# A hybrid scan and attention kernel: other order in the head, a shifted pipeline in the scan loop, a fourth lane and fewer background steps at the end

## Chip, core and metric

The kernel runs on one core of one Trainium2 chip. Times are device microseconds (us) of one execution. A few executions of each kernel are taken, and the median is quoted with its range.

## The reference, cut to what matters

The input is four images of 64 x 64 positions with 96 channels. One layer takes signs of the inputs, projects, convolves 3 x 3, and runs a selective scan over the 4096 positions of an image in four directions, for 192 channels with 16 states each. A small attention and a quantised feed-forward part follow. The scan, simplified:

```python
delta = softplus(delta + delta_bias)
def step(h, inp):
    ut, dt, Bt, Ct = inp
    dA = exp(dt[..., None] * A)                       # decay
    h = dA * h + (dt * ut)[..., None] * Bt[:, :, None, :]   # injection
    y = einsum('bkdn,bkn->bkd', h, Ct)                # product, sum over the states
    return h, y
```

## The kernel before

The scan is cut into 1536 pieces of 128 rows (32 channels x 4 states) by 1024 positions: 4 images, 4 directions, 4 stretches of positions, 24 pieces for each. For a piece ScalarE (ACT) computes the decay, GpSimd (POOL) the injection, VectorE (DVE) the scan, DVE or POOL the product with C, and TensorE (PE) sums over the states. A tally of the microseconds given to DVE and POOL, kept when the program is built, decides which of them takes a product. SyncE (SP) issues nearly all loads and stores. This is the loop:

```python
AHEAD = 4
...
self.decay(0)
for i in range(AHEAD):
    self.inject(i)
for i in range(n):
    ...
    if i + 1 < n:
        self.decay(i + 1)                       # ACT
    if i % 8 == 3 and i > 8:
        self.evacuate(i - 4)                    # ACT: ys <- yp, then stores
    if i >= 3:
        self.reduce(i - 3)                      # PE: sums of y, three steps behind
    if i + AHEAD < n:
        self.inject(i + AHEAD)                  # POOL, four steps ahead; 9 buffers
    self.late_product()                         # POOL: product of piece i - 1
    self.scan(i)                                # DVE (and its product)
    ...
    if i % 8 == 3 and self.todo:
        ...
        lanes.append(self.prepare())            # delta of later pieces: PE, ACT, DVE, store
    interleave(lanes)
    next(back, None)                            # one step of background work
    if i > n - 64:
        next(back, None)                        # a second one near the end
```

`back` is background work in small steps: the next image's head (projections, convolution, rows), a transposition, and the epilogue of an image whose scans are done.

Three stretches run without a loop to fill them. The **head** is the first image's column sums, projections, convolution (16 parts), the rows that hold B, C and the signs, and the first deltas. The **tail** is the last image's epilogue: eight chunks of sums, of which some were done in the background, a small middle, and eight closing chunks in three lanes. A lane is a set of buffers in which one chunk is worked on beside those of the other lanes.

```python
more = [e.spare_lane(x) for x in range(2)]
drain([behind] + [e.sums(ln) for ln in more])
drain([e.middle()])
drain([e.last(ln) for ln in [e.lane] + more])
```

The signs (gT) that a preparation multiplies are loaded ahead, except for the first direction of the next image:

```python
if (b, k) not in self.gs:
    self.load_signs(b, k)                       # loaded where it is used
if (ci, part) == (NCH - 1, 0) and k != KORD[-1]:
    self.load_signs(b, KORD[KORD.index(k) + 1]) # loaded 24 pieces ahead
```

## Time and profile before

5511.64 us, median of three runs (5508.68 to 5516.53). The page of the profiled run begins with the busy time of each engine and its share of the span:

```profile
PE 3466.0 (63%) x20089; PEld 1360.3 (25%) x20089; DVE 4996.1 (91%) x3142; ACT 3631.0 (66%) x5673; POOL 4947.3 (90%) x2247
```

The groups of instructions between 280 and 5140 us show the work of one piece (line, engine, operation, tiles, count; busy us in all, mean ns of one; idle time before them by releaser):

```profile
L421 POOL TENSOR_TENSOR w<-dl,bc 128x1024 f32<-128x1024 f32 x1471 | 3429.1, 2358 | 72.3 <-PE yp L1409 51.0 <-issue 8.6 <-DMA bc<-bcd 8.4
L421 DVE TENSOR_TENSOR_SCAN dA<-dA,cy,w 128x1024 f32<-128x1024 f32 x691 | 1618.9, 2343 | 86.7 <-ACT dA L1336 71.5 <-ACT cy L1378 9.8 <-POOL w L421 5.2
L421 DVE TENSOR_TENSOR w<-dA,bc 128x1024 f32<-128x1024 f32 x928 | 1136.7, 1225 | 53.0 <-DVE dA L421 0.5 <-DMA bc<-bcd 0.3
```

Both engines are busy nine tenths of the span. The prediction works from these durations.

| stretch of the profiled run | us |
|---|---|
| head, to the first injection | 260.9 |
| to piece 96 | 582.0 |
| pieces 96 to 1440 | 4450.1 |
| pieces 1440 to 1535 | 349.8 |
| piece 1535 to the end | 122.3 |

A piece's time is read off as follows, here and below: the busy time of ACT's decays is summed in windows of 4 us, and piece N is where N/1536 of it is reached. This is good to some 2 us.

### The profile page before, as it was taken

To read this page: it belongs to the slowest core of one execution; us is meant where nothing else is said; L and a number is where in the kernel's file an instruction comes from. 1 tells how busy PE (TensorE), PEld (TensorE's weight loads), DVE (VectorE), ACT (ScalarE), POOL (GpSimd) and SP (SyncE) were. 2 spreads that over 40 slices of the span, in tenths; PEclk is the share of its full clock that TensorE was granted. 3 is DMA by queue.
4 is the path that set the end of the run, shared out by engine and by line. 5 is a ranking of instruction groups with operands and counts; after the bars stand their busy time and mean duration, and the time that the engine had idled before them with its cause. 6 is when DMAs were issued, how large, how long until landed. Compare 5 with 4: busy or idle time off the path is not lost. (4 is left out here: it accounts for less than half of the span.)

```text
span 5504.2 us, 62064 instructions
## 1 busy us (share of the span) xinstructions
PE 3466.0 (63%) x20089; PEld 1360.3 (25%) x20089; DVE 4996.1 (91%) x3142; ACT 3631.0 (66%) x5673; POOL 4947.3 (90%) x2247
## 2 busy tenths in 40 slices
PE   5456765467655776656665677664777664444677
PEld 2221222122222232222222222221232221111223
DVE  3299999999999999999999999999999999999884
ACT  4468776677766667777767666775656775655544
POOL 2199999899999999999999999999999999999981
PEclk7666876578867777768876787766787665556777
DMA  4455665766666666676765666666666565765642
GB/s 78 122 184 195 206 203 188 245 214 208 209 200 202 195 205 211 201 235 212 219 192 185 207 211 195 205 217 225 198 209 203 178 198 196 219 204 185 203 152 60
DMA packets 613659, 1069.84 MB, mean 194 GB/s; under 512 B 225147, under 2 KB 344468, under 8 KB 611540
## 3 DMA queue, kind: packets, MB, share of 16 engines
q1 hardware_dynamic: 612244, 1065.86, 61.3%
q8 instruction: 157, 2.57, 0.2%
q14 instruction: 170, 1.39, 0.1%
q10 hardware_dynamic: 1088, 0.02, 0.0%
HBM read 833.16 MB, written 229.35 MB: 193 GB/s over the span
## 5 line engine op out<-in xcount | busy, mean ns | idle before, releaser
L421 POOL TENSOR_TENSOR w<-dl,bc 128x1024 f32<-128x1024 f32 x1536 | 3580.9, 2358 | 155.5 <-PE yp L1409 72.6
L1336 ACT ACTIVATE dA<-dl,anm 128x1024 f32<-128x1024 f32 x1536 | 1714.5, 1116 | 474.4 <-DVE w L421 285.8
L421 DVE TENSOR_TENSOR_SCAN dA<-dA,cy,w 128x1024 f32<-128x1024 f32 x726 | 1700.9, 2343 | 90.7 <-ACT dA L1336 75.5
L1409 PE MATMUL yp<-w,sum 128*32 128x256 f32 x12288 | 1286.6, 514 | 384.8 <-POOL w L421 230.7
L421 POOL TENSOR_TENSOR w<-h,bc 128x1024 f32<-128x1024 f32 x573 | 1349.1, 2355 | 124.1 <-DVE h L421 110.0
L421 DVE TENSOR_TENSOR w<-dA,bc 128x1024 f32<-128x1024 f32 x963 | 1179.5, 1225 | 54.7 <-DVE dA L421 0.5
L421 DVE TENSOR_TENSOR_SCAN h<-dA,cy,w 128x1024 f32<-128x1024 f32 x426 | 996.7, 2340 | 16.0 <-ACT dA L1336 15.8
L1409 PEld LDWEIGHTS yp<-w,sum 128*32 128x32 f32 x12288 | 315.6, 128 | 1467.9 <-issue 690.1
L1378 ACT COPY cy<-dA 128x1 f32<-128x1 f32 x721 | 113.5, 157 | 772.5 <-DVE w L421 770.6
L421 DVE TENSOR_TENSOR_SCAN dA<-dA,w 128x1024 f32<-128x1024 f32 x237 | 540.9, 2282 | 36.7 <-ACT dA L1336 28.4
L1271 PE MATMUL dps<-gT,wdz 128*128 128x64 fp8e5 x1000 | 113.9, 313 | 358.8 <-ACT ys L1423 329.8
L421 DVE TENSOR_TENSOR_SCAN h<-dA,w 128x1024 f32<-128x1024 f32 x147 | 334.8, 2278 | 4.9 <-ACT dA L1336 3.4
L1284 PE MATMUL dps<-sp,ident 128*128 128x512 f32 x376 | 273.0, 815 | 46.0 <-ACT dps L1280 45.8
L1414 PE MATMUL yp<-ya,back 128*128 128x256 f32 x576 | 235.1, 528 | 4.5 <-DMA ya<-yd 2.5
L659 PE MATMUL cv<-tp,cwA 128*96 128x512 fp8e5 x576 | 198.4, 470 | 60.3 <-ACT r L706 55.1
L1271 PEld LDWEIGHTS <-wdz 128*128 128x128 fp8e5 x1024 | 95.4, 152 | 440.1 <-issue 409.7
L1271 PE MATMUL dps<-gT,wdy 128*128 128x64 fp8e5 x504 | 58.5, 317 | 205.2 <-ACT ys L1423 203.2
L1276 ACT ACTIVATE pd<-dps,dbias,pvd 128x512 f32<-128x512 f32 x188 | 143.3, 762 | 20.2 <-PE dps L1271 20.2
L1414 PEld LDWEIGHTS yp<-ya,back 128*128 128x128 f32 x576 | 122.6, 246 | 133.4 <-issue 93.5
L1378 ACT COPY cy<-h 128x1 f32<-128x1 f32 x431 | 79.9, 185 | 113.7 <-DVE h L421 112.8
L941 PE MATMUL yc<-eys,mean 96*96 96x512 f32 x240 | 132.1, 702 | 24.2 <-DVE vks L421 8.9
L1277 ACT ACTIVATE sp<-dps,dbias,pvd 128x512 f32<-128x512 f32 x188 | 144.2, 767 | 0.0
(312 smaller groups left out, 4433.1 us busy)
## 6 DMA issues: line engine op xcount, KB each, us to landing
dl<-dld SPq DMA_DIRECT2D x768, 512.0 KB
bc<-bcd SPq DMA_DIRECT2D x512, 512.0 KB
dld<-pd SPq DMA_DIRECT2D x125, 512.0 KB
yd<-ys SPq DMA_DIRECT2D x768, 64.0 KB
dld<-pd SPq DMA_DIRECT2D x126, 256.0 KB
ya<-yd SPq DMA_DIRECT2D x192, 128.0 KB
pu<-ud SPq DMA_DIRECT2D x32, 512.0 KB
pu<-utd SPq DMA_DIRECT2D x30, 512.0 KB
```

What stands on the lines that cost most here:

```text
L421: return getattr(self.eng, name)(out, *args, **kw)
L659: nc.tensor.matmul(ps, w[:, 96 * h : 96 * h + 96], tp[:, 8 * q + dy : 8 * q + dy + 8, dx : dx + IW], start=(w is taps[0][1]), stop=(w is t ...
L941: self.c.nc.tensor.matmul(ps, w, x, start=(i == 0), stop=(i == len(pairs) - 1))
L1271: nc.tensor.matmul(pv[:, s], wd[:, k, s], gT[:, :, c0 : c0 + 16], start=(s == 0), stop=(s == 7))
L1276: nc.scalar.activation(d[:, 0], ps, AF.Abs, scale=sc, bias=bi)
L1277: nc.scalar.activation(t, ps, AF.Relu, scale=sc, bias=bi)
L1284: nc.tensor.matmul(ps, c.ident, t, start=False, stop=True, skip_group_check=True)
L1336: c.nc.scalar.activation(t, self.dlt[i // NQ][0], AF.Exp, scale=c.anm[:, g, NQ * KORD[e] + q : NQ * KORD[e] + q + 1])
L1378: self.c.nc.scalar.copy(self.carries[g, q], h[:, CH - 1 : CH])
L1409: c.nc.tensor.matmul(y[32 * x : 32 * x + 32, g % 2, :], c.sum4, prod[:, 256 * x : 256 * x + 256], start=(q == 0), stop=(q == NQ - 1 and no ...
L1414: c.nc.tensor.matmul(y[:, g % 2, :], w, src, start=False, stop=(n == len(more) - 1))
```

## The change

It touches all stretches. In the head: small loads move later and to another queue, the second read-out of x goes to DVE, convolution parts go line by line with a PSUM tile each, the transposed rows xr are laid clear of the column buffers, DVE takes half of the copies, and the first deltas are broadcast from SBUF instead of through DRAM. In the loop: three injections ahead instead of four, and sums four steps behind instead of three, with the loads, copies and preparations that belong to it one step later. At the end: one background step per piece to the last, a fourth closing lane, the last two products on DVE; the loads of the tail's sums change their order, and the first product of the middle goes to DVE.

```diff
-AHEAD = 4
+AHEAD = 3
...
         for t in gTs + [wdz]:
             nc.gpsimd.memset(t.bitcast(F32), 0.0)
+        yield
... (12 loads of sbR leave ACT, 24 of anm move; both are issued by SP after the weights)
-                nc.scalar.activation(t, ps, AF.Identity, bias=c.bo)
+                if alone:
+                    nc.vector.tensor_scalar(t, ps, c.bo, None, ALU.add)
...
+            if alone:
+                parts = [(h, q) for q in range(NQ8) for h in range(2)]
...
-                    ps = (two[0][:, at : at + 512] if alone else bank("cv" + nm, 0))[0:96]
+                    if alone:
+                        ps = c.p.dA.tile([128, CH], F32, name=f"cv{nm}_{b}", tag="dA")[0:96, 0:512]
...
         with tc.tile_pool(name=f"rw_{b}", bufs=1) as rw:
+            xrs = rw.tile([128, 96, 64], BF16, name=f"xr_{b}", tag="xr")
... (scan loop)
-            if i % 8 == 3 and i > 8:
-                self.evacuate(i - 4)
-            if i >= 3:
-                self.reduce(i - 3)
+            if i % 8 == 4 and i > 8:
+                self.evacuate(i - 5)
+            if i >= 4:
+                self.reduce(i - 4)
...
             next(back, None)
-            if i > n - 64:
-                next(back, None)
... (scan, end)
+        pool = c.vec.us + 1.2 > c.gps.us + 2.4 and i < len(self.pieces) - 2
...
     drain([behind] + [e.sums(ln) for ln in more])
+    more.append(e.fourth_lane())
... (start of the scans)
+        for n in range(3):
+            for x in range(2):
+                r = p.dl.tile([128, CH], F32, name=f"dl{x}_s{n}", tag=f"dl{x}")
+                nc.sync.dma_start(r, w[x][32 * n : 32 * n + 32].unsqueeze(1).to_broadcast([32, 4, CH]))
```

## The prediction

> **What bounds the kernel now.** I read the busy table of the page first: of the span of 5504.2 us, VectorE (DVE) is busy 4996.1 and GpSimd (POOL) 4947.3, TensorE (PE) and ScalarE (ACT) about two thirds. From the groups I take the durations: a piece of the scan (1536 of them) is one POOL injection of 2.358 us, one DVE scan of about 2.34 and one product, 1.225 us on DVE or 2.355 on POOL. The work is dealt out between the two engines when the kernel is built, so both bound the loop together. Then I cut the span at the first injection (260.9 us) and near the end of the last scan (5390), with the windows view:
>
> ```profile
> core 0: us, PE busy (x) PEld busy (x) DVE busy (x) ACT busy (x) POOL busy (x), PEclk, DMA share, GB/s
> 280.00:5140.00 4860.00, 3058.75 (x18276) 1169.72 (x18277) 4657.32 (x2773) 3316.18 (x5167) 4679.74 (x2038) 0.71 0.64 205
> 5140.00:5390.00 250.00, 185.03 (x869) 75.92 (x868) 206.35 (x133) 127.86 (x198) 205.34 (x93) 0.75 0.49 154
> 5390.00:5504.00 114.00, 81.03 (x260) 35.96 (x259) 50.98 (x95) 52.37 (x88) 1.17 (x3) 0.75 0.23 65
> 0.00:260.90 260.90, 137.54 (x659) 76.59 (x660) 73.41 (x138) 127.41 (x209) 41.96 (x107) 0.74 0.44 95
> ```
>
> The loop runs at 96.3% of POOL (4679.7 of 4860): at most 180 us are to be had there. Its last 250 us run at 82%. The head (260.9 us) and the tail (114 us) bound no engine: they are chains of waits. The change touches all four stretches; the total is their sum, since they follow one another.
>
> Where the head waits, ACT in its first 90 us, then ACT and PE from 90 to 260 us (waiter, releaser: us in all, times, longest):
>
> ```profile
> ACT slab L277 <- DMA sbR<-in_sl_dt: 15.3, 1, 15.3
> ACT sz L600 <- DMA szd<-sz: 12.2, 1, 12.2
> ```
> ```profile
> ACT r L706 <- DVE v L703: 19.8, 10, 2.9
> ACT sg L641 <- DVE cz L421: 10.7, 11, 1.3
> ACT xr L740 <- DMA utd<-ut: 10.2, 1, 10.2
> ```
> ```profile
> PE cv L659 <- ACT r L706: 32.2, 14, 3.7
> ```
>
> And the start of the scans, in the timeline (start, length):
>
> ```profile
> 246.22 3.09 SPq L440 DMA_DIRECT2D dld<-w_s  x4
> ...
> 253.90 4.84 SPq L1313 DMA_DIRECT2D dl<-dld  x6
> ...
> 260.93 13.84 POOL L421 TENSOR_TENSOR w<-dl,bc 128x1024 f32<-128x1024 f32 x6 [57.84 <-DMA dl<-dld]
> ...
> 268.72 0.69 DVE L421 TENSOR_TENSOR w_s<-dA_s,pu_s 128x512 f32<-128x512 f32 x1 [22.33 <-DMA pu_s<-utd]
> ...
> 271.15 4.47 DVE L421 TENSOR_TENSOR_SCAN h<-dA,w 128x1024 f32<-128x1024 f32 x2 [1.74 <-ACT dA L1336]
> ```
>
> Delta goes to DRAM at 246 and comes back at 261; the first scan waits to 271, because ACT holds the first decay behind a copy that needs a late load (268.7).
>
> **What the Trainium skill says.** "PSUM — Partial Sum Buffer", section "PSUM bank collisions raise a hardware error": two engines may not touch one bank and quadrant at once, two reads included. The trace agrees: r (ACT) and v (DVE) read the same convolution bank, and r starts as v ends (v 180.84 + 0.80, r 181.67). The same page, "Engine vs sequencer instructions": the queues of ACT, DVE and POOL are strict first-in first-out. That is the decay behind the copy above. "DMA: Bandwidth & Descriptors", "Issuing engines are not separate DMA queues": moving a DMA to another engine saves only issue time. Here that is not small: 17 of the tiny loads of anm kept SP issuing for 12.96 us, 0.76 each. "TensorE: Matmul & The Clock Gate", "What's actually happening": the clock is either half or full. The convolution's matmuls of 512 columns come 0.215 or 0.43 us apart in the trace.
>
> **The change, part by part.**
>
> *Before the convolution.* The 12 loads of sbR leave ACT (it waits 15.3 us on them, and PE holds the column sums behind the weights' transposes until 17.8 us); a yield puts the sums first; the second read-out of x goes from ACT to DVE; signs of z go to larger buffers and are stored four at a time, which ends the 12.2 us wait. The column sums come maybe 10 us earlier, but the weights still arrive in SP order (wl at 24 us, its signs at 33.2 now, perhaps 28), so I let only 5 of that through: first convolution matmul at 53 us, not 71.2: -18. But SP gets the 12 + 24 small loads (12 x 0.37 + 24 x 0.76 = 22.7 us of issue) in the second convolution part, in front of the stores that free the eight small buffers (5 used per part). Those give some 1.5 parts, 11 us, of slack, and landing costs 2: I charge +9.
>
> *Convolution*, 71.2 to 194.1 us, 123 us for 16 parts. Each part gets its own PSUM tile, so PE no longer waits for r of the part before (32.2 us). But where PE runs fast, the period is set by ACT and DVE: 5.64 us between 134.9, 140.56 and 146.2 (r 0.78, two DVE steps 1.6, sign, exp, ln, exp 2.4, u and v 1.45), and a projection adds 1.5 to 2.3 us. Old: 6 parts with two projections (9.4) and 10 without: 113. New: 12 with one (7.5) and 4 without: also 113. So only the excess over 113 can go, 8 of 10 us: -8. Order by lines makes six column stores, not four, each followed by 6.0 us in which SP gets nothing out; two now fall at the very end.
>
> *Rows.* xr is laid where it need not wait for the column store (10.2 us), but that late store also delays the last signs: I take -3. Half of the copies and one of two read-outs go to DVE; PE then paces (1.1 us a bank against 1.34): -2.
>
> *Start.* Two parts of delta stay in SBUF and are broadcast from there: transposes done 231, PE 2-3 us, eight ACT steps 5.2, DVE 2.8 gives 241, and one pair of loads of 512 KB some 5 (estimate from 7 us for the six at 253.9): injection at 246 instead of 261 (-15), first scan at 249 instead of 271 (-22). Both engines share the work: -18. Head in all: -18+9-8-3-2-18 = -40.
>
> *Loop.* What the engines wait for between 280 and 5140 us:
>
> ```profile
> POOL w L421 <- DVE h L421: 96.5, 114, 3.7
> POOL w L421 <- PE yp L1409: 52.2, 38, 6.9
> ```
> ```profile
> DVE dA L421 <- ACT dA L1336: 99.9, 71, 7.1
> ```
> ```profile
> PE yp L1409 <- POOL w L421: 214.2, 99, 7.2
> ```
>
> Sums one step later end most of PE's waits for products (214 us), so what stands behind them in PE's queue, and then in ACT's, comes earlier; the 99.9 and 52.2 are consequences of such queues. Yet the injection's buffer is still freed by a sum issued two steps earlier (9 buffers; 4 ahead and 3 behind became 3 and 4, so between sum and injection nothing is gained), and DVE has one injection less in hand. The waits for ACT where ACT has too much (background prologues) stay. A chosen tenth of the 180: -20.
>
> *Last pieces and tail.* With one background step per piece instead of two, 205.3 us of POOL work at the 95% of a stretch with an epilogue (1400 to 1600: 190.2 of 200) takes 216, not 250: -34, of which I take -28, as other work stays. The price: an epilogue chunk takes 11 to 13 steps, so the last 62 pieces finish five of the six chunks available; three are left for three lanes where two were left. The two took 5394.5 to 5426.5, 32 us with PE busy most of it: +7. The eight closing chunks take three rounds now (5428.8 to 5504, 75 us); four lanes make two. PE is busy 15.4 of each 20 us there, some 57 of 75, so I count 63: -12. Last two products on DVE: -2. Sum -35.
>
> Total -40 -20 -35 = -95: 5511.6 - 95 = 5417.
>
> **Rivals.** (a) The head keeps its length: SP becomes its bound. By my count it issues 16 x 2.2 + 6 x 6.6 + 22.7 = 97 us within a convolution of 113; for it speaks that every store waits in this one queue; then the head gives -15 and the time is 5442. (b) The loop gets worse: with three injections in hand, POOL, held up by a late sum, starves DVE (now only 7.7 us). It would show in "DVE <- POOL w"; +30 us, 5467. Against it: three steps are 10 us, longer than the longest wait of 6.9. (c) The loop gets much better, since PE's blocked queue was the root of most stalls: half of the 180 us, 5347, over 2% faster. For it: 214 us of waiting on PE is the largest wait that the shift addresses; against: PE is off the path most of the time. (d) The end gives half: PE is the tail's bound, and the leftover chunk eats more than the lane saves: 5434.
>
> **Range and chances.** The head may give 15 to 65, the loop +20 to -70, the end -10 to -50; taken as independent that is about 32 us either side for one standard deviation, so 5376 to 5460 for 8 in 10. Faster by 2% needs -110, half a deviation beyond my centre: 0.3. Slower by 2% would need every part to fail: 0.01.
>
> **What would show it.** First convolution matmul near 53 us; "PE cv <- ACT r" gone and a period still over 5.6 us; a stop on store landing in the third or fourth part; first injection about 223, first scan three after. In the loop "PE yp <- POOL w" far below 214 and POOL's share up by less than 1%. In the last 250 us POOL above 90%; three chunks in the tail's sums, two rounds after, tail near 110 us. I am wrong if the head stays above 245, if the loop's idle time moves by more than 70 us, or if the last pieces still run at 82%.

## More of the kernel before

The calls ran on different chips of one kind; each had the kernel before beside it, with medians from 5512.5 to 5513.8.

## The result

The changed kernel takes 5478.56 us (median of four, 5475.02 to 5484.12), the kernel before beside it 5512.47 (four runs). The ratio is 0.9939, 95% interval 0.9922 to 0.9956: -34 us, where -95 was predicted, and outside the predicted range. A ratio here is the mean time of one kernel's runs over that of the other's of the same rounds, so not quite the ratio of the medians.

The busy times of the page are almost those of before (DVE 5016.3 us, POOL 4938.7), as they must be when the work is the same.

The windows of the changed kernel answer to the first fence of the prediction (window; its length, busy us of PE, PEld, DVE, ACT, POOL; clock, DMA share, GB/s):

```profile
280.00:5140.00 4860.00, 3010.04 (x18164) 1166.57 (x18156) 4631.54 (x2758) 3299.10 (x5138) 4649.65 (x2026) 0.72 0.65 204
5140.00:5390.00 250.00, 186.60 (x883) 74.75 (x884) 221.39 (x154) 135.70 (x211) 204.47 (x95) 0.80 0.52 164
0.00:235.30 235.30, 129.94 (x651) 71.87 (x651) 90.56 (x163) 110.91 (x182) 41.95 (x107) 0.71 0.48 92
```

The head is 25.6 us shorter (235.3 instead of 260.9). POOL's busy time in the loop's window fell, from 4679.74 to 4649.65 of 4860 us. The end of the second window lies past the last piece now, so it must be read by pieces:

| stretch of the profiled run | before | after | difference |
|---|---|---|---|
| to the first injection | 260.9 | 235.3 | -25.6 |
| to piece 96 | 582.0 | 563.7 | -18.3 |
| pieces 96 to 1440 | 4450.1 | 4472.0 | +21.9 |
| pieces 1440 to 1535 | 349.8 | 314.2 | -35.6 |
| piece 1535 to the end | 122.3 | 132.4 | +10.1 |

These add to -22, not -34: the profiled run of the kernel before (5506) was faster than its median, that of the changed one (5484) its slowest of four. The loop's +21.9 is partly an accident, as the experiments show.

In the head, the waits of the changed kernel up to 90 us, then from 90 to 240 us (waiter, releaser: us in all, times, longest):

```profile
PE xps L574 <- DVE xb L566: 9.3, 3, 8.6
```
```profile
ACT r L729 <- DVE v L726: 19.9, 13, 1.9
ACT xr L765 <- DMA utd<-ut: 12.3, 1, 12.3
PE xa L760 <- DMA xg<-sg: 15.3, 1, 15.3
PE cv L682 <- ACT r L729: 4.4, 7, 1.2
ACT sg L662 <- DMA ud<-u: 1.9, 2, 0.9
```

PE's wait for r is down from 32.2 to 4.4 us, as intended, but what sets the period, ACT's r behind DVE's v, is the same 19.9 as before (19.8). The wait for the store of signs, charged with +9, is 1.9. And xr, laid clear of the column buffers, waits for their store all the same. The timeline shows it (start, length, engine, operation, idle time before and its releaser):

```profile
188.25 0.58 ACT L765 CAST xr<-xa 128x512 bf16<-128x512 f32 x1 [12.32 <-DMA utd<-ut]
188.29 0.12 POOL L832 MEMSET g<- 128x32 f32 x1 [10.48 <-DMA utd<-ut]
188.31 0.69 DVE L765 CAST xr<-xa 128x512 bf16<-128x512 f32 x1 [11.61 <-DMA utd<-ut]
...
235.32 9.26 POOL L423 TENSOR_TENSOR w<-dl_s,bc 128x1024 f32<-128x1024 f32 x4 [46.81 <-DMA dl_s<-w_s]
237.69 4.60 DVE L423 TENSOR_TENSOR_SCAN h<-dA,w 128x1024 f32<-128x1024 f32 x2 [5.38 <-POOL w L423]
...
251.29 2.29 DVE L423 TENSOR_TENSOR_SCAN h<-dA,w 128x1024 f32<-128x1024 f32 x1 [8.42 <-POOL w L423]
```

Three engines start within 0.06 us after one store, and their tiles are different ones. At the bottom, the third scan starts 13.6 us after the first and waits 8.4 of them for POOL.

In the loop, the waits from 280 to 5140 us, first of the kernel before (the line that the prediction did not show), then of the changed one:

```profile
PE yp L1409 <- ACT pd L1290: 76.6, 37, 4.7
```
```profile
PE yp L1462 <- ACT pd L1343: 230.3, 55, 8.1
DVE dA L423 <- ACT dA L1389: 116.6, 89, 9.4
POOL w L423 <- DVE h L423: 109.0, 118, 5.6
PE yp L1462 <- POOL w L423: 58.9, 21, 9.3
POOL w L423 <- PE yp L1462: 50.8, 36, 6.2
```

PE's wait for POOL's products fell from 214.2 to 58.9, as foretold. Its wait for the copy pd rose from 76.6 to 230.3. The largest waits of the engines that bound the loop, POOL and DVE, hardly fell or rose (96.5 to 109.0, 99.9 to 116.6, 52.2 to 50.8).

### The profile page after: what moved, and what is told of

It reads as the page before. It is cut to its first block, busy times and chain, and to the rows that moved or that the text cites.

```text
span 5482.3 us, 62080 instructions
## 1 busy us (share of the span) xinstructions
PE 3415.9 (62%) x20083; PEld 1355.4 (25%) x20083; DVE 5016.3 (91%) x3171; ACT 3615.3 (66%) x5648; POOL 4938.7 (90%) x2245
## 5 line engine op out<-in xcount | busy, mean ns | idle before, releaser
L1462 PE MATMUL yp<-w,sum 128*32 128x256 f32 x12288 | 1254.7, 505 | 323.8 <-ACT pd L1343 235.0
L1324 PE MATMUL dps<-gT,wdz 128*128 128x64 fp8e5 x1008 | 116.6, 316 | 399.9 <-ACT ys L1476 373.9
L423 DVE TENSOR_TENSOR_SCAN h<-dA,w 128x1024 f32<-128x1024 f32 x143 | 325.9, 2279 | 18.8 <-POOL w L423 16.1
L1467 PEld LDWEIGHTS yp<-ya,back 128*128 128x128 f32 x576 | 117.6, 236 | 119.9 <-issue 88.2
```

The source lines that it names most:

```text
L423: return getattr(self.eng, name)(out, *args, **kw)
L1324: nc.tensor.matmul(pv[:, s], wd[:, k, s], gT[:, :, c0 : c0 + 16], start=(s == 0), stop=(s == 7))
L1462: c.nc.tensor.matmul(y[32 * x : 32 * x + 32, g % 2, :], c.sum4, prod[:, 256 * x : 256 * x + 256], start=(q == 0), stop=(q == NQ - 1 and no ...
L1467: c.nc.tensor.matmul(y[:, g % 2, :], w, src, start=False, stop=(n == len(more) - 1))
```

## The experiments

Fourteen kernels ran, each in five rounds with the kernel before (four to six executions of each), all correct. The stretches are of each one's profiled run; before, in the calls, had medians of 5512.7, 5513.4, 5513.8 and 5512.6.

| kernel | median us | ratio | piece 96 at | 96 to 1440 | 1440 to 1535 | rest |
|---|---|---|---|---|---|---|
| before | 5512.5 | 1 | 582.0 | 4450.1 | 349.8 | 122.3 |
| changed | 5478.6 | 0.9939 | 563.7 | 4472.0 | 314.2 | 132.4 |
| no_loop | 5475.5 | 0.9938 | 564.1 | 4459.8 | 314.3 | 132.0 |
| loop_only | 5494.8 | 0.9972 | 575.8 | 4455.8 | 336.4 | 121.7 |
| end_only | 5486.7 | 0.9958 | 581.9 | 4463.2 | 310.9 | 134.2 |
| head_only | 5497.8 | 0.9978 | 565.8 | 4466.6 | 344.8 | 126.5 |
| no_end | 5497.7 | 0.9973 | 564.0 | 4468.8 | 341.1 | 123.2 |
| two_steps | 5492.2 | 0.9969 | 563.9 | 4467.9 | 336.2 | 119.9 |
| no_fourth | 5480.2 | 0.9941 | 563.7 | 4464.5 | 313.7 | 137.7 |
| head_waits | 5458.5 | 0.9902 | 552.6 | 4468.4 | 311.3 | 129.3 |
| signs_early | 5463.1 | 0.9910 | 564.0 | 4451.5 | 314.1 | 128.9 |
| tail_more | 5472.4 | 0.9923 | 562.6 | 4476.7 | 313.5 | 122.4 |
| head_more | 5454.8 | 0.9897 | 548.0 | 4465.8 | 312.2 | 128.6 |
| all_edits | 5430.3 | 0.9851 | 548.6 | 4449.5 | 311.9 | 122.2 |
| all_no_loop | 5420.3 | 0.9831 | 545.4 | 4430.3 | 311.1 | 130.5 |
| all_old_sums | 5440.9 | 0.9870 | 546.1 | 4453.8 | 310.8 | 128.3 |

### One part at a time

My first theory (A) was that the loop part costs the 22 us; the rivals were that it is neutral and the shift of the head costs them (B), or that it gives what I predicted (C).

**no_loop**: the changed kernel with the loop part undone.

```diff
-AHEAD = 3
+AHEAD = 4
-            if i >= 4:
-                self.reduce(i - 4)
+            if i >= 3:
+                self.reduce(i - 3)
... (loads, copies, preparations back by one step)
```

> The changed kernel with its loop part undone (four injections ahead, sums three behind, the order of loads, copies and preparations as before); head and end stay changed. Measured so far: changed minus before is -24 us at piece 24, -18 at piece 96, +4 at piece 1440, -32 at the last piece and -22 at the end of the profiled spans. Theory A (the loop part itself costs the 22 us between pieces 96 and 1440): that stretch returns from 4472 to about 4450 us, and the time falls from 5478.6 to about 5456. Rival B (the loop part is neutral; the loss is a worse meeting of the background work with the pieces, because the head ends earlier and hands over a different rest of the first prologue): 4470 and 5478. Rival C (the loop part gives what I predicted, -20, and the head's shift costs 40): 4490 and 5498.

Measured 5475.49 (0.9938, 0.9924 to 0.9952), pieces 96 to 1440 in 4459.8 us. Theory A, as I put it (5456), falls: beside the head and the end the part changes nothing that five rounds can see.

**loop_only**: the kernel before with the same edit the other way round.

> The kernel before with the loop part alone. Theory A: pieces 96 to 1440 take some 22 us more than the 4450 of before, and the time is some 15 to 22 us above before, 5530. Rival B: within 5 us of before, 5512. Rival C: 5492, as predicted.

Measured 5494.77 (0.9972, 0.9960 to 0.9985), -15 us. That is close to the predicted -20, but it does not come from where I had put it: pieces 96 to 1440 take 4455.8, as in the kernels without it, and pieces 1440 to 1535 take 336.4 instead of 349.8. Why these got shorter is not shown. Of the profiled run's gain a further 5.4 us are chance: the first injection comes at 255.5, not 260.9, though no instruction before it differs.

**end_only**: the kernel before with the end part alone.

```diff
+        pool = c.vec.us + 1.2 > c.gps.us + 2.4 and i < len(self.pieces) - 2
...
-            if i > n - 64:
-                next(back, None)
...
+    more.append(e.fourth_lane())
```

> The kernel before with the end part alone: one background step per piece to the end, the fourth lane, two last products on DVE, the order of the loads, the first product of the middle on DVE. From the two traces the last 96 pieces gave -36 and what follows the last product +10: 5486. If these gains need the loop part (sums one step later) to show, 5500 or more; if they are what I predicted, 5477.

Measured 5486.71 (0.9958, 0.9946 to 0.9971): the -26 that the two traces had shown. This run gave something more. Up to piece 1472 its instructions are those of the kernel before, yet its trace reaches piece 1440 at 5045.1 us, 13 us later than the trace of before (5032.1). So two traces of the same instructions differ by 13 us over this stretch, and of the +21.9 most may be such a difference. In the head these two runs agree within 1 us up to piece 24, but loop_only, with the same head, has its first injection 5.4 us earlier. The eight traces with the head of the changed kernel have it between 235.3 and 236.0. So a single trace settles a question of 10 us in the head, but not over 4450 us of loop.

**head_only**: the changed kernel with loop and end parts undone.

> The changed kernel with loop part and end part both undone: the head alone. Theory A: the head's -24 us at piece 24 stays to the end, 5488. Rival B: the shift loses it again by piece 1440, 5505 to 5512. As predicted (-40): 5472.

Measured 5497.78 (0.9978, 0.9966 to 0.9991), -12 to -15 us by ratio and by median, of 16 us at piece 96. This lies between the theories; the expected 5505 to 5512 of rival B is not what came.

Alone, the three parts give -15, -12 and -23 by their ratios, together -50; the change gives -34. Where is the overlap?

**no_end**: head and loop together, the end undone.

> The changed kernel with its end part undone: head and loop parts together. Alone, the head gave 0.9978 of before (-12 us), the loop 0.9972 (-15), the end 0.9958 (-23): -50 in sum, but all three give 0.9939 (-34), and head and end without the loop also -34. Theory O (overlap in the last pieces: the loop part alone shortened pieces 1440 to 1535 from 350 to 336 us, and with the end part, which brings them to 314, nothing of that is left): head and loop add up here, 5483 to 5487, with pieces 1440 to 1535 at about 336. Rival B (the loop part loses between pieces 96 and 1440 once the head ends earlier): 5497 or more, as for the head alone, with that stretch some 15 us longer than in the kernels whose loop is unchanged. Those took 4450.1 (before), 4463.2 (end alone), 4466.6 (head alone) and 4459.8 (no loop part): one code, four traces, 16 us apart; so a difference of one trace to another of under 16 us there proves nothing.

Measured 5497.73 (0.9973, 0.9960 to 0.9986): the two do not add up in time, as rival B said. But its stretch 96 to 1440, 4468.8, is only 2 us longer than that of the head alone (4466.6), and the last pieces took 341.1, nearer to theory O's 336 than to the 350 of before. So neither theory holds as written: by the time, the loop part adds nothing beside the new head, and no one stretch shows where.

**two_steps**: the changed kernel with the second background step of the last pieces back.

```diff
             next(back, None)
+            if i > n - 64:
+                next(back, None)
```

> The changed kernel with two background steps in each of the last 63 pieces again, nothing else undone. If the one step per piece is what brought pieces 1440 to 1535 from 350 to 314 us, they go back to about 336 (as with the loop part alone), no chunk is left for the sums at the end, what follows the last product shortens by some 8 us, and the time is about 5492. Rival: the two products moved to DVE and the earlier sums brought it; then pieces 1440 to 1535 stay near 314 and the time falls to 5470, since the left-over chunk is gone.

Measured 5492.19 (0.9969, 0.9954 to 0.9984), the last pieces in 336.2 us and the rest in 119.9. The last pieces and the time are as expected to the microsecond; the rest shortened by 12 us, not 8. The one step per piece is what shortens the last pieces by 22 us, at a price of 12 in the tail.

**no_fourth**: the changed kernel with three closing lanes.

```diff
-    more.append(e.fourth_lane())
```

> The changed kernel without the fourth lane: three closing rounds of three, three and two chunks. I predicted -12 us for two rounds instead of three; the traces of before and after show the closing rounds at 72 and 64 us, but the start of the lanes later by some 5 us, for ten loads of 0.42 us of issue each now stand in one queue. If the lane is worth the 8 us less the 5, the time is 5482; if the lane gives the full 12, 5490; if PE is the bound and it gives nothing, 5478.

Measured 5480.15 (0.9941, 0.9928 to 0.9954). The rest after the last piece is 137.7 instead of 132.4 us in the traces; the times differ by 2 us, less than their spread. The lane is worth 5 us by the traces and nothing that the times can tell, not the predicted 12.

### The waits in the head, the stops at the signs, the tail

**head_waits**: two edits in the head of the changed kernel.

```diff
-        with tc.tile_pool(name=f"rw_{b}", bufs=1) as rw:
-            xrs = rw.tile([128, 96, 64], BF16, name=f"xr_{b}", tag="xr")
+        with tc.tile_pool(name=f"xr_{b}", bufs=1) as xrp, tc.tile_pool(name=f"rw_{b}", bufs=1) as rw:
+            xrs = xrp.tile([128, 96, 64], BF16, name=f"xr_{b}", tag="xr")
... (the second xr likewise)
         self.decay(0)
+        c.vec.us = c.gps.us = 0.0
         for i in range(AHEAD):
```

> The changed kernel with two edits in the head. First, the transposed rows xr get a memory pool of their own. In the trace ACT, DVE and POOL all start at 188.25 to 188.31 us after waiting for the column store, though the addresses of xr lie clear of the column buffers: theory, the wait belongs to the pool of the rows as a whole, which overlaps the column buffers, and with a pool of its own xr starts when its transposes are there, at 183: the transposed deltas' start and the first injection come 5 us earlier (230 instead of 235.3). Rival: the wait is real for xr, and nothing moves. Second, the two engines' tallies start at zero. The third scan waits 8.4 us for POOL (251.3 instead of 242.3), because the tally, which still counts the head's work on DVE, gives the first three products to POOL, which has three injections to do first. Theory: with the tallies at zero these products go to DVE, the third scan starts within 6 us of the first, and piece 24 (322.1 in the changed kernel) is reached 5 us earlier still: 312 for both edits. Rival: POOL's injections bound the start anyway and piece 24 gains only what the first edit gives, 317. The time: 5469, or 5474.

Measured 5458.46 (0.9902, 0.9886 to 0.9918). The timeline:

```profile
182.94 0.69 DVE L765 CAST xr<-xa 128x512 bf16<-128x512 f32 x1 [5.94 <-PE xa L760]
...
230.58 9.26 POOL L423 TENSOR_TENSOR w<-dl_s,bc 128x1024 f32<-128x1024 f32 x4 [41.75 <-DMA bc<-bcd]
232.96 2.30 DVE L423 TENSOR_TENSOR_SCAN dA<-dA,w 128x1024 f32<-128x1024 f32 x1 [5.17 <-POOL w L423]
...
240.49 2.29 DVE L423 TENSOR_TENSOR_SCAN dA<-dA,w 128x1024 f32<-128x1024 f32 x1
```

The first copy of xr starts at 182.94, not 188.25, and waits for its transposes alone, at the same addresses as in the changed kernel (203424 to 215712 in both built programs; the column buffers begin at 216288). So the wait belonged to the pool that xr shared with tiles which do overlap the column buffers. The third scan follows 7.5 us after the first, not 13.6. Piece 24 is reached at 312.1, as expected. The time fell by 20, more than the 10 us of the head; the other 10 are of the size of the spread between calls and single traces, and I do not explain them.

**signs_early**: the changed kernel, with the signs of the next image loaded 24 pieces ahead.

```diff
+        nb = (b + 1, KORD[0])
+        if ci == NCH - 1 and k == KORD[-1] and b + 1 < NB and nb not in self.gs and (b + 1, KORD[0] % 2) in c.ready:
+            self.load_signs(*nb)
```

I had seen the stop in the traces of both kernels. In the changed one, near piece 356:

```profile
1447.31 1.04 PE L1324 MATMUL dps<-gT,wdz 128*128 128x64 fp8e5 x8 [12.25 <-DMA gT<-gTd]
1453.11 2.37 POOL L423 TENSOR_TENSOR w<-dl,bc 128x1024 f32<-128x1024 f32 x1 [10.11 <-issue]
1454.65 2.36 DVE L423 TENSOR_TENSOR_SCAN dA<-dA,cy,w 128x1024 f32<-128x1024 f32 x1 [9.39 <-ACT dA L1389]
```

PE waits 12.25 us for the load. The sums behind it in PE's queue are late, and then POOL (10.11) and DVE (9.39) stand too. The label "issue" in POOL's line says only that the profile shows no releaser; it is the same stop.

> The changed kernel with one more load ahead: the signs of the next image's first direction are loaded with the last four lines of pieces of this one, 24 pieces before their first use; so far they are loaded in the step that uses them. In all ten traces so far TensorE stands still three times (pieces 356, 740, 1124) for this load, 23.5 to 30.7 us in all between 560 and 5040 us, and the eight pieces around each take 28 to 40 us where eight others take 26. Theory S (in those stops ACT, DVE and POOL stop too, and where the three stops meet the queues is what makes the loop part gain or lose some 10 us from trace to trace): the wait is gone, the three stretches of eight pieces take 26 to 27 us each, 97.7 us in the changed kernel becomes 79, and the time is 5462. Rival: the stop is slack that comes back elsewhere, 5474 or more.

Measured 5463.07 (0.9910, 0.9897 to 0.9923). The waits for the load are gone; the three stretches of eight pieces take 28.0, 26.1 and 27.8 us, 82 instead of 98. Pieces 96 to 1440 take 4451.5, where seven traces with the same loop and the new head (in three of them with edits) take 4464.5 to 4476.7. The gain is real, 15 us by the medians. The kernel before has the same stops (97.7 us for these three stretches), so it should gain as well; that was not run. The stops do not explain why the loop part gave nothing.

**tail_more**: three edits in the end of the changed kernel.

```diff
-    drain([behind] + [e.sums(ln) for ln in more])
-    more.append(e.fourth_lane())
+    e.rest = e.rest[::-1]
+    sums = [behind] + [e.sums(ln) for ln in more]
+    interleave(sums)
+    c.later.tick()
+    lasts = [e.last(e.fourth_lane())]
+    next(lasts[0])                       # its loads
+    drain(sums)
+    for ln in [e.lane] + more:
+        lasts.append(e.last(ln))
+        next(lasts[-1])                  # their loads, before the middle
     drain([e.middle()])
-    drain([e.last(ln) for ln in [e.lane] + more])
+    drain(lasts)
... (scan loop)
-            next(back, None)
+            if i < n - 3:
+                next(back, None)
```

It starts from these lines of the changed kernel's timeline:

```profile
5356.99 6.76 PE L994 MATMUL yc<-eys,mean 96*96 96x512 f32 x8 [2.67 <-DVE vks L423]
5363.68 1.93 PE L1462 MATMUL yp<-w,sum 128*32 128x256 f32 x32
5375.07 1.96 PE L994 MATMUL ln0ps<-ln0b,on 96*96 96x512 f32 x4 [1.00 <-DMA ln0b<-yd]
```

The last sums (5363.68) stand behind 6.76 us of the left-over chunk, and the spare lanes start at 5375, 18 us after the last product; before, it was 9.5.

> The changed kernel with three edits in the end: the background stops for the last three pieces, so that the last sums do not stand behind the left-over chunk in TensorE's queue (5.4 us in the trace of the kernel without loop part); the closing chunks are taken in the order in which they were stored, not in the reverse one, which began with the one stored last; the loads of the closing lanes are issued before the middle, those of the fourth lane before the sums end. Theory: the lanes start 4 us earlier and all four are loaded when the middle ends, not 11 us after the sums: 5 to 10 us, 5471. Rival (the closing is bound by TensorE's work alone, 84% busy in a round): the loads come earlier, but only the 4 us of the sums are gained, 5475.

Measured 5472.36 (0.9923, 0.9911 to 0.9936); the rest after the last piece is 122.4 instead of 132.4. The ten microseconds are there in the traces (the times fell by 6, which is within their spread), but not where I put them. From the last piece to the middle it is 53.8 us (5352.8 to 5406.6) against 54.4 (5349.9 to 5404.3): the sums start earlier and last longer, since the left-over chunk now runs beside the two others. From the middle to the end it is 68.6 us against 78.0. So the loads, which I had thought the smaller term, gave nearly all; their other order and their earlier issue are not told apart. With them, two closing rounds took 62.8 us from the first lane's first matmul to the last matmul (5408.5 to 5471.3), where the changed kernel took 71.0 (5407.5 to 5478.5).

**head_more**: the edits of head_waits, the read-out of x back on ACT, and buffers of its own for the second half of the rows.

```diff
-                if alone:
-                    nc.vector.tensor_scalar(t, ps, c.bo, None, ALU.add)
-                else:
-                    nc.scalar.activation(t, ps, AF.Identity, bias=c.bo)
+                nc.scalar.activation(t, ps, AF.Identity, bias=c.bo)
... (tb2: two tiles of another pool for gh == 1; the signs are stored first)
```

> The two edits of head_waits and two more in the head: the read-out of x goes back from DVE to ACT (PE waited 9.3 us for it behind DVE's sums over the convolution weights, which wait for loads), and the second half of the rows is written to buffers of its own, with the signs stored first (DVE waited 3.98 us, from 201.7 to 205.7, for the store of the first half). Theory: first convolution matmul at 50 instead of 56.2, signs' transposes 4 us earlier, first injection at 221 instead of 231; piece 24 at 302 where head_waits had 312; time 5449. Rival (loads of the weights set the start of the convolution whatever ACT does): only the 4 us of the rows, 308 and 5454.

Measured 5454.75 (0.9897, 0.9884 to 0.9910). The first convolution matmul is at 53.58 (expected 50), the signs' copy at 205.2 (210.2 in head_waits), the first injection at 224.9, piece 24 at 306.5. Each term came at about half its size: moving the read-out gave 2.6 of the 6 us, since the weights come next (PE's wait for those that POOL prepares rose from 4.6 to 8.7 us).

**all_edits**: signs_early, tail_more and head_more in one kernel.

> All edits of the three other kernels of this call together. If they add up, from 5478.6: head -29, loop -17, end -7: 5425. If the gain of the head is again given back in the loop by a third, as from piece 24 to 1440 in the traces, 5435.

Measured 5430.26 (0.9851, 0.9838 to 0.9863): halfway between the two figures. By the medians the three kernels gave 15, 6 and 24 us alone, 45 in sum, and 48 together, so the edits add up within the spread; that a part of the head's gain is given back is not excluded.

### What the loop part is worth

With the stops gone, the loop part was taken out of this kernel (**all_no_loop**, the diff of no_loop) and, separately, only its later sums (**all_old_sums**: the same diff without the line of AHEAD).

> The kernel with all edits (5430) without the loop part of the change: four injections ahead, sums three behind, loads, copies and preparations at the old steps. Theory N (the part is neutral: TensorE's waits for products were off the path, and they only change their name): 5430 within 6 us, pieces 96 to 1440 again 4450. Theory P (the prediction: later sums relieve TensorE and through it ACT and POOL): 5445 or more. Rival Q (three injections ahead and later sums cost, as the longer stretch of the four traces with new head and new loop, 4468 on average against 4463, might say): 5420 or less.

> The kernel with all edits, three injections ahead as in it, but sums three behind and all loads, copies and preparations at the old steps. Theory N: 5430 again. If the two halves cancel (later sums gain some 15, one injection less in hand loses some 15): 5445, slower than both others. If one injection less in hand were harmful by itself, VectorE's waits for POOL's injections and POOL's for sums would rise above the some 4 and 35 us that they take in the kernel with all edits.

Measured, in one call: all_no_loop 5420.30 (5418.51 to 5423.15; 0.9831, 0.9817 to 0.9846), all_old_sums 5440.89 (5440.82 to 5444.19; 0.9870, 0.9854 to 0.9886). Between them lies only the number of injections ahead: four instead of three are worth 21 us. The kernel with all edits (5424.98 to 5434.01, of another call) lies between, so sums one step later win back about 10 of the 21, across two calls. By the traces only 4 of these lie in the loop (4449.5 us instead of 4453.8) and 6 after the last piece (122.2 instead of 128.3); why there is not shown. The waits from 550 to 4990 us show it, first of all_no_loop, then of all_old_sums:

```profile
POOL w L423 <- DVE h L423: 89.1, 104, 2.5
POOL w L423 <- PE yp L1484: 44.1, 30, 5.6
```
```profile
POOL w L423 <- DVE h L423: 140.9, 141, 5.3
POOL w L423 <- PE yp L1484: 10.0, 6, 3.2
```

POOL's queue holds, for a piece, the injection AHEAD steps on and then the late product of the piece before, which needs DVE's scan. With one injection less in front, POOL comes to that product earlier and waits for the scan: 140.9 us instead of 89.1. It waits less for a free buffer (10.0 instead of 44.1). In all it waits 151 us instead of 133 for the two, and the loop from piece 96 to 1440 takes 4453.8 us instead of 4430.3. With the later sums, in all_edits, the two waits are 102.0 and 35.4. POOL's busy time between these pieces is 4279 to 4280 us in all three, so what differs is its waiting. So rival Q is right for this kernel, and the two halves partly cancel, as the second expectation had it, but unequally. That the injections alone cost as much in the changed kernel was not run.

all_no_loop, 5420.30 us, is the best kernel: 0.9831 of the kernel before, and 58 us below the changed kernel by the medians.

## Why the prediction was wrong

The predicted -95 was -40 for the head, -20 for the loop and -35 for the end. By the kernels with one part and by the traces it became about -16, zero or a loss, and -25.

**Head, -40 predicted.** The first injection came 25.6 us earlier (the old head's three traces spread by 5), and 18.3 were left at piece 96.

- Before the convolution (-18): the first matmul at 56.2 instead of 71.2, -15. Nearly right; the read-out put on DVE took 2.6 of the rest.
- The small loads (+9): nothing. My count of what SP issues was right (24 loads took 16.25 us), but the buffers gave more slack than I charged; the wait is 1.9 us.
- Convolution (-8): the step "only the excess over 113 can go, 8 of 10 us" failed: next to nothing went. From its first matmul to the last u it took 122.2 us and takes 120.5; two more traces of the old head have 121.2 and 117.7. The period is set by ACT and DVE, as I said: r waits for v 19.9 us where it was 19.8, which fits the Trainium skill, "PSUM — Partial Sum Buffer", section "PSUM bank collisions raise a hardware error". From the last u to the first transpose of the rows 0.7 us became 5.3, so in all +3. The last signs are stored at 178.95, after SP has stood for 6.02 us behind a column store, and PE waits 15.3 us for them (`xg<-sg` above). I had named these 6 us and the two stores at the very end, and counted them at nothing.
- Rows (-3 and -2): from the first transpose to the signs 37.0 us became 34.6, so -2.4. The step "xr is laid where it need not wait for the column store" failed: the wait was for the pool, and head_waits gave it back, 5.3 us. The step "PE then paces" failed too: tbc on DVE and sgn on ACT read the same bank one after the other, and the pair of banks takes 2.84 us where it took 2.68.
- Start (-18): from the signs to the injection 29.8 us became 18.8, so -11, and the first scan came 33.5 us earlier. This part was not kept. I wrote "both engines share the work: -18" and left the tally out of account, which gives POOL the first three products just when POOL is behind. head_waits showed the cost: piece 24 at 312.1 instead of 322.1, of which 5 were the rows.

**Loop, -20 predicted.** The step that failed is "a chosen tenth of the 180". The mechanism was half right: sums one step later ended most of PE's waits for products (214.2 to 58.9 us), and in the last experiment they are worth about 10 us, of which 4 in the loop. What I weighed wrongly is the other half, "DVE has one injection less in hand". I looked for its cost in DVE's waits for POOL and in rival (b), and these stayed small (7.7 us before, 6.6 in the changed kernel). The cost is in POOL's own waits for DVE's scans, since the injections in hand are also what POOL does while it waits: 21 us in the kernel with all edits. Beside the old head and end the part gave -15, in the profiled run most of it in the last pieces (13) and some by chance before the first injection (5); beside the new ones it gave nothing. Why its gain there does not last beside the new head alone (no_end) stays open; the difference, 12 us, comes from three ratios that are each uncertain by some 7 us, and no stretch shows it clearly.

**End, -35 predicted, -23 to -26 measured.** The last pieces were better than foretold: -36 instead of -28. The tail was worse: +10 instead of -7 (sums +7, rounds -12, products -2). The left-over chunk cost +9 in front of the middle, close to the +7, but by standing in PE's queue ahead of the last sums, not by being a third chunk. The fourth lane's -12 failed, but not by the step "PE is busy some 57 of 75, so I count 63": counted from the fourth lane's first matmul two rounds took 63.6 us where three took 71.4, and with earlier loads (tail_more) 62.8 from the first lane's. What I left out is the start: 11 us went by between the last sums and the fourth lane's first matmul, in which the loads of all lanes stood in one queue and began with the chunk that had been stored last.

**The ranges.** The first injection was expected at 223 and came at 235; POOL in the last 250 us above 90% was right, once the loop's end is taken (17.6 to 20 of each 20 us from 5140 to 5340). "I am wrong if the loop's idle time moves by more than 70 us" was a bad sign to choose: it moved by 30 (POOL's 4679.7 to 4649.7) although the forecast failed, and half of that can be one trace against another.

## What to carry to other kernels

When two engines share a loop, an item "in hand" for one of them is also what the other has to do while it waits; look for the cost of taking it away in both engines' waits. Before explaining a difference between two traces, find out by how much two traces of the same instructions differ: here 13 us over the 4450 of the loop, and 5 us within the first 261. A wait that everything seems to have in common (three engines starting within 0.06 us) belongs to something they share, here a memory pool, and the cheapest gains lay in such waits: a load issued where it is used, a pool, a tally that starts wrong, the order and the time of the last loads.

## What the Trainium skill lacked or had wrong

- "DMA: Bandwidth & Descriptors", "Issuing engines are not separate DMA queues", takes the time of issue for small beside the DMA itself. It does not say that many issues add up in one queue: here 24 small loads kept the queue's engine issuing for 16.25 us, and another order and an earlier issue of the closing loads were worth some 9 us (78.0 to 68.6 from the middle to the end); but where buffers had slack, as in the convolution, the 16 us cost only 1.9 us of waiting.
- No page has that a tile may wait for others of its pool: xr waited until 188.25 us for a store whose buffer it did not overlap, and started at 182.94 at the same addresses with a pool of its own.
- "PSUM — Partial Sum Buffer", "Engine vs sequencer instructions", has the queues of ScalarE, VectorE and GpSimd as strict first-in first-out and TensorE's matmuls in program order, and the traces agree; what it does not say is how far one late load reaches: a 12.25 us wait of TensorE stopped GpSimd for 10.11 and VectorE for 9.39 us.
- No page gives the spread of a long kernel: the kernel before ran between 5501 and 5523 us, and two traces of the same instructions differed by 13 us in the loop and by 5 in the head.
